# Segment sums of the first eleven tiles moved beside the FFN, their left factors moved into the steps, and the first ten steps reordered

## The chip, the cores and the metric

The kernel runs on one core of a Trainium2 chip. The metric is device time in microseconds: the median of several executions. A separate execution is profiled, and every row quoted here is from that one. The engines are called TensorE (PE, its weight loads PEld), VectorE (DVE), ScalarE (ACT), GpSimd (POOL) and SyncE (SP, which only issues transfers).

## The reference

One layer of a recurrent model for x of 4 batches, 256 positions and 512 features. xn is the layer norm of x. The mixer projects xn with in_proj_w to a gate (8192 wide), to xBC (8192 + 2 x 1024) and to dt (128 heads). xBC goes through a causal convolution of four taps and a silu. Then, with heads of 64 and eight groups that share B and C:

```python
dt = softplus(dt + dt_bias); Adt = -exp(A_log) * dt
L = exp(segment_sum(Adt))            # decay from position j to position i
Y_diag = (C B^T * L) @ (x * dt)      # inside a chunk
Y_off = C @ states * exp(cumsum(Adt))  # from the chunk before
y = (Y_diag + Y_off + D * x) * silu(gate)
y = group_rms_norm(y) * norm_w
out = x + (y @ out_proj_w.T) * silu(FFN(xn))
```

The FFN has ternary weights of width 1792 with a scale for each row. The kernel uses chunks of 128 positions, two for each batch, in place of the reference's 32, which gives the same sums. `segment_sum` of a head is a running sum of Adt from each key position to each later query position.

## The kernel before

The work has two stages in program order: a front, and then 66 steps.

**The front** (`front`) makes the layer norm, the FFN, dt with its sums, and B and C with their scores for the eight groups. The FFN is the backbone: 28 FFN steps (two halves of the tokens by fourteen blocks of 128 features), each with 8 gate matmuls, 8 up matmuls and 8 down matmuls; the down matmuls are those of the FFN step before. Everything else is cut into pieces of generators, and the loop takes one piece, `next(pieces)`, at three places of each FFN step. One such call is a turn: 84 turns lie in the FFN, and what is left over runs after it. `all_pieces` says which generator starts at which turn. `dt_pieces` starts at turn 6; it writes the rows of Adt (`rows`, in DRAM) at turn 17. `bc_pieces(g)`, the projection chain of a group, starts at turn 11 + 8g and has 14 pieces, so two chains overlap. In its first four pieces four matmul products add into one PSUM bank `px`, and after each ScalarE copies the bank into `cpad` or `xpad` (L424) before the next product may add. Later pieces add `pz` and `pq` (L434, L437, L440), and then VectorE runs three convolution taps on `cT` and three on `bT` (L181), which read `cpad` and `xpad`; the copies of the next chain wait for these reads. Pieces 11 to 13 make the scores (L460) that go to DRAM. `early_pieces` starts at turn 20. For each of eleven tiles it loads two blocks of in_proj_w, makes four sums of 128 x 256 from them in two turns (L142 to L146, the left factors of a Strassen-like product) and stores them in DRAM in `early`; one tile takes five turns.

FFN results leave through `hl` (L565, a VectorE difference that the next down matmuls need), `sg` (L548), and `ffn_out` (L301, L302).

**The steps.** Step i (0 to 65) projects tile i (of 64, two heads each), while tile i - 1 goes through the state-space part and tile i - 2 through gating; from step 10 on (`og >= 0`) the output projection of an earlier group runs in it too, three or four products a step (L721). The projection is seven products of four matmuls of 128 x 512 (L173) in PSUM banks `px`, `pq` and `pz`, which several products share: `px` is copied by ScalarE (`pz` L822, `gT` L832, `xpad` L846 and L877) between products, and `pq` is added to `xpad` by VectorE (L869) before its second product may add to it.

For tile i - 1, two rows of Adt are loaded with a broadcast to 128 partitions (`load_rows`, tiles `m` of 128 x 1024). Each is turned into the segment sums by one VectorE scan (`decay_scan`, L612), exponentiated on ScalarE (`decay_exp`, L615) and multiplied by the scores (`meet`, L618 and L619). `y_begin` (L651) puts D * x in the bank `py`; `values_0` and `values_1` transpose x (L624) and scale it (v0 and v0t at L632, v1 at L641); `y_products` (L665) is 48 small matmuls in 12 pairs. `last_tap` (L177, ScalarE) and three taps (L181) make the convolution of tile i, `conv_silu` its silu. `yg` (L672) gates tile i - 2, and `Square` (L857, L860) feeds the norm.

The scans of step i are one in the middle of the step and one at its end. In steps 0 to 10 the left factors of the next tile are read from `early` (transfers L803 and L914); from step 11 on `combine_w` makes them at the end of the step with four sums.

Nothing is scheduled by a planner: inside `tc.manual_schedule()` each engine runs its instructions in the order of the program. SP issues the transfers in program order too, and waits in place when a transfer needs a result or a free buffer; POOL issues the accumulating transfers and casts the FFN weights.

Of the kernel before, what the change touches and what calls it, by code (L numbers as in the profile page):

```python
# [81 lines left out]
def mixer_ffn(ctx: ExitStack, tc: tile.TileContext, x, in_w, conv_w, conv_b, dt_bias, a_log, d_col,  # L82
# [101 lines left out]
    def conv_silu(i, xT):  # L184
        xf = xT.rearrange("p b l -> p (b l)")
        nc.scalar.activation(xf, xf, AF.Silu, bias=cb[:, i:i + 1])


    def front(pre, one_of, fp, f2, hp, wq):
        ones = one_of.tile([P, P], F32, name="ones")  # L190
# [384 lines left out]
    with (tc.manual_schedule(), tc.tile_pool(name="pre", bufs=NT) as pre,  # L575
          tc.tile_pool(name="one_of", bufs=1) as one_of, tc.tile_pool(name="fp", bufs=3) as fp,
          tc.tile_pool(name="f2", bufs=2) as f2, tc.tile_pool(name="hp", bufs=1) as hp,
          tc.tile_pool(name="wq", bufs=1) as wq):
        a = front(pre, one_of, fp, f2, hp, wq)

# [14 lines left out]
    def load_rows(ct):  # L595
        ms = []
        for h in range(2):
            m = mp.tile([P, T], F32, name="m")
            nc.sync.dma_start(m, rows[2 * ct + h, 0:T].partition_broadcast(P))
            ms.append(m)  # L600
        return ms

    def load_off(ct):
# [5 lines left out]
        return offs  # L609

    def decay_scan(m):
        nc.vector.tensor_tensor_scan(m, m, after, 0.0, ALU.add, ALU.mult)  # L612

# [40 lines left out]

    def y_products(ps, vs, ms, offs):
# [4 lines left out]
        for b in range(NB):  # L660
            py = ps[b // 2][:, b % 2, :]
            for q, v, stop in ((0, v0, True), (1, v1, False), (1, v0t, True)):
                for h, d in enumerate(halves):
                    m = off[h][:, b, :] if v is v0t else diag[h][:, b, q, :]
                    nc.tensor.matmul(py[d, q * P:(q + 1) * P], v[:, b, h, :], m,  # L665
                                     start=False, stop=stop, skip_group_check=True)

# [93 lines left out]
    with tc.manual_schedule():  # L761
        nc.sync.dma_start(gm, scores[0])
        ms, offs = {0: load_rows(0)}, {0: load_off(0)}
        xTs, gTs, yps, wos, rights, toms = {}, {}, {}, {}, {}, {}
        sqacc = rs = ya = outs = left = nxt = ob = sa = sb = sc = None
        for i in range(CT + 2):
# [62 lines left out]
            if here:  # L829
# [3 lines left out]
                if lead:  # L833
                    decay_exp(ms[i - 1][1])
                if i:
                    decay_scan(ms[i][0])
                product(pz, a12, x21, False)
            if old:
                meet(ms[i - 1][0], offs[i - 1][0])
                meet(ms[i - 1][1], offs[i - 1][1])  # L840
                if r == 0 and here:
                    nc.sync.dma_start(gm, scores[g])
                yps[i - 1] = y_begin(i - 1, xTs[i - 1])
            if here:
                product(px, s3, t3, False)
                nc.scalar.copy(xpad_h[1], by_batch(px))  # L846
# [6 lines left out]
            if older:  # L853
                yf = yg.rearrange("p b l -> p (b l)")
                if (i - 2) % PER_G == 0:
                    sqacc = sqp.tile([P, T], F32, name="sqacc")
                    nc.scalar.activation(sqacc, yf, AF.Square)  # L857
                else:
                    sq = sqp.tile([P, T], F32, name="sq")
                    nc.scalar.activation(sq, yf, AF.Square)  # L860

# [13 lines left out]
            if here:  # L875
                product(px, a22, t4, False)
                nc.scalar.copy(xpad_h[0], by_batch(px))  # L877
                if i == 0:
                    decay_scan(ms[i][0])
                    decay_scan(ms[i][1])  # L880
                product(pq, s4, x22, False)
            if old and og < 0:
                vs.append(values_1(i - 1, xTs[i - 1]))
            if here:
                nc.vector.tensor_add(gT[:, HALF:], gT[:, HALF:], pq)  # L885
                if og >= 0 and on == 0:
                    rs = small.tile([P, NT], F32, name="rs2", bufs=2)
                    nc.vector.reciprocal(rs, sd)
            if old and og >= 0:
                vs.append(values_1(i - 1, xTs[i - 1]))  # L890
            if here:
                xTs[i] = xtp.tile([P, NB, L], F32, name="xT")
# [7 lines left out]
            if old:  # L900
                y_products(yps[i - 1], vs, ms.pop(i - 1), offs.pop(i - 1))
            if older and (i - 2) % PER_G:
# [132 lines left out]
```

## Time and profile before

| what | us |
|---|---|
| runs: median (lowest to highest of 3) | 1793.18 (1792.14 to 1793.36) |
| the profiled execution's own time | 1795.49 |
| its span, first to last instruction | 1793.0 |
| TensorE busy in the span | 1742.7 (97%) |
| VectorE busy in the span | 1448.6 (81%) |
| ScalarE busy in the span | 1066.0 (59%) |
| the 128 scans `m<-m,after`, VectorE | 292.0, 2282 ns each |

A group row reads: line, engine, operation, out<-in, shape, count, then busy us and the mean ns of one, then the engine's idle time before it and who ended it. A row of waits reads: who waited, for whom, us in total, times, longest. A row of stretches reads: from:to, length, then for PE, PEld, DVE, ACT and POOL the busy us and number of instructions, then the granted TensorE clock (1.00 is full), the busy share of the DMA engines and GB/s. A timeline row reads: start us, length us, engine, line, operation, tiles, shape, count, and in brackets the idle time before it and what ended it. The stretches of the steps are cut in the middle of each step's first product.

### The profile page before, as it was taken

Reading aid. Unit: us, or ns where it says so; the run is one execution under the profiler, and the core shown is the slowest. Engines: PE = TensorE matmul, PEld = TensorE weight load, DVE = VectorE, ACT = ScalarE, POOL = GpSimd, SP = SyncE. Lnnn points to the kernel's source line nnn. Section 1 sums busy time; section 2 is a strip of 40 time slices with the busy share of each in tenths; the row PEclk is TensorE's granted clock in tenths of the full one; section 3 lists DMA queues with packets and bytes.
Section 4 is the critical chain, followed back from the end, with each engine's and each line's share of the span. In section 5 each row is a group of like instructions: output and inputs, shape, how many; then the busy total and the mean of one; then the engine's idle time right before and its main releaser. Section 6 shows DMA issues by size and latency. Waiting matters only on the chain.

```text
span 1793.0 us, 22592 instructions
## 1 busy us (share of the span) xinstructions
PE 1742.7 (97%) x8494; PEld 1117.4 (62%) x8494; DVE 1448.6 (81%) x1740; ACT 1066.0 (59%) x1417; POOL 197.3 (11%) x239
## 2 busy tenths in 40 slices
PE   9999999999899999999999999999999999999989
PEld 6566666455466666666666666666666666666667
DVE  5758675799988888888888888888888888888846
ACT  4544343577666666666666666666666666666630
POOL 3221221000000000111011101110111011101110
PEclk9999999999999999999999999999999999999989
DMA  6254643566846665767676767676777676766674
GB/s 223 80 185 155 212 162 123 196 223 215 253 138 203 195 210 178 201 197 210 180 202 197 210 182 203 197 208 185 203 197 209 185 203 197 208 185 203 179 211 141
DMA packets 164235, 342.69 MB, mean 191 GB/s; under 512 B 15392, under 2 KB 55968, under 8 KB 164128
## 3 DMA queue, kind: packets, MB, share of 16 engines
q1 hardware_dynamic: 141296, 287.78, 46.3%
q0 software_dynamic: 22832, 53.49, 16.8%
q8 instruction: 67, 1.10, 0.2%
q14 instruction: 40, 0.33, 0.1%
HBM read 236.08 MB, written 76.28 MB: 174 GB/s over the span
## 4 chain that ended last, share of the span: by engine, by line
PE 89%; DVE 6%; ACT 4%; issue 1%; DMA 1%; ACTq 0%; DVEq 0%; SPq 0%
PE px L173 27%; PE po L721 21%; PE pq L173 13%; PE py L665 9%; PE pz L173 7%; PE pp L285 4%; PE pf L293 2%; ACT xpad L846 2%; PE tp L624 2%; PE pg L460 1%; DVE cT L181 1%; PE pv L683 1%; DVE xT L181 1%; DVE bT L181 1%; DVE m L612 0%
## 5 line engine op out<-in xcount | busy, mean ns | idle before, releaser
L173 PE MATMUL px<-xc,w 128*128 128x512 f32 x576 | 278.7, 606 | 19.4 <-ACT xpad L846 14.1
L612 DVE TENSOR_TENSOR_SCAN m<-m,after 128x1024 f32<-128x1024 f32 x128 | 292.0, 2282 | 0.0
L181 DVE SCALAR_TENSOR_TENSOR xT<-xpad,cw,xT 128x1024 f32<-128x1024 f32 x192 | 246.2, 1282 | 4.6
L173 PEld LDWEIGHTS px<-xc,w 128*128 128x128 f32 x576 | 104.2, 190 | 136.3 <-issue 97.4
L721 PE MATMUL po<-wo,ya 128*128 128x256 f32 x768 | 178.4, 382 | 0.0
L665 PE MATMUL py<-m,v 128*64 128x128 f32 x2048 | 162.2, 278 | 3.9 <-DVE v L641 3.9
L618 DVE TENSOR_TENSOR m<-m,gm 128x1024 f32<-128x1024 f32 x128 | 154.8, 1209 | 8.9 <-ACT m L615 8.9
L721 PEld LDWEIGHTS po<-wo,ya 128*128 128x128 f32 x768 | 142.6, 192 | 17.6 <-issue 0.3
L904 POOL DMA_DIRECT2D sqacc<-sq x55 | 46.9, 853 | 931.1 <-ACT sq L860 927.3
L173 PE MATMUL px<-xc,s 128*128 128x512 f32 x288 | 137.5, 600 | 5.0 <-ACT pz L822 2.2
L173 PE MATMUL px<-xnT,w 128*128 128x512 f32 x288 | 141.9, 615 | 0.0
L173 PE MATMUL pq<-xnT,s 128*128 128x512 f32 x288 | 136.2, 595 | 1.1 <-DVE xpad L869 1.1
L615 ACT ACTIVATE m<-m 128x1024 f32<-128x1024 f32 x128 | 135.4, 1058 | 0.7
L173 PE MATMUL pq<-xc,s 128*128 128x512 f32 x288 | 135.4, 592 | 0.3 <-DVE gT L885 0.3
L173 PE MATMUL pz<-xnT,w 128*128 128x512 f32 x288 | 135.3, 592 | 0.0
L665 PEld LDWEIGHTS py<-m,v 128*64 128x64 f32 x2048 | 118.0, 138 | 26.2 <-issue 19.7
L721 PE MATMUL po<-tw,sy 128*128 128x256 f32 x512 | 117.1, 382 | 1.2 <-ACT sa L775 1.2
L869 DVE TENSOR_TENSOR xpad<-xpad,pq 128x512 f32<-128x512 f32 x64 | 43.7, 683 | 80.3 <-ACT xpad L846 80.3
L721 PEld LDWEIGHTS po<-tw,sy 128*128 128x128 f32 x512 | 98.1, 192 | 15.2 <-ACT sa L775 1.6
L624 PEld LDWEIGHTS tp<-ident,xT 128*128 128x128 f32 x512 | 64.3, 143 | 67.8 <-issue 67.2
L672 DVE TENSOR_TENSOR yg<-py,gT 128x512 f32<-128x512 f32 x128 | 83.8, 678 | 22.7 <-PE py L665 22.7
L173 PEld LDWEIGHTS px<-xc,s 128*128 128x128 f32 x288 | 54.7, 192 | 73.0 <-issue 65.8
(172 smaller groups left out, 3059.8 us busy)
## 6 DMA issues: line engine op xcount, KB each, us to landing
m<-rows SPq DMA_DIRECT2D x128, 512.0 KB, 6.4
w<-in_in_w SPq DMA_DIRECT2D x133, 256.0 KB, 6.8
mo<-rows SPq DMA_DIRECT2D x128, 256.0 KB, 7.2
gated<-yg SPq DMA_DIRECT2D x64, 512.0 KB, 8.2
ya<-gated SPq DMA_DIRECT2D x30, 1024.0 KB, 7.1
sqacc<-sq POOLq DMA_DIRECT2D x55, 512.0 KB, 5.4
wo<-in_out_w SPq DMA_DIRECT2D x64, 256.0 KB, 7.1
acc<-sa POOLq DMA_DIRECT2D x24, 512.0 KB, 5.9
```

Of the source, the lines that this page charges most:

```text
L173: nc.tensor.matmul(pp, a[:, k, :], b[:, k, :], start=start and k == 0, stop=k == KT // 2 - 1, skip_group_check=not start)
L181: nc.vector.scalar_tensor_tensor(xT, xpad[:, :, k:k + L], cw[:, i, k:k + 1], xT, ALU.mult, ALU.add)
L285: nc.tensor.matmul(pp, w[:, k * P:(k + 1) * P], part[:, k, :], start=(k == 0 and part is xh), stop=(k == KT - 1 and part is xl))
L612: nc.vector.tensor_tensor_scan(m, m, after, 0.0, ALU.add, ALU.mult)
L615: nc.scalar.activation(m, m, AF.Exp)
L618: nc.vector.tensor_mul(m, m, gm[:, 0:T])
L624: nc.tensor.transpose(tp[:, b, :], xT[:, b, c * P:(c + 1) * P], ident)
L665: nc.tensor.matmul(py[d, q * P:(q + 1) * P], v[:, b, h, :], m, start=False, stop=stop, skip_group_check=True)
L672: nc.vector.tensor_mul(yg[:, 2 * i:2 * i + 2, :], ps[i], by_batch(gT[:, i * HALF:(i + 1) * HALF]))
L721: nc.tensor.matmul(po, a[:, k, :], b[:, k, :], start=start and k == 0, stop=k == HG - 1, skip_group_check=not start)
L869: nc.vector.tensor_add(xpad_h[1], xpad_h[1], by_batch(pq))
L904: nc.gpsimd.dma_start(sqacc, sq, accum_op=ALU.add)
```

## The change

`early` now holds 22 tiles of 128 x 1024: the segment sums of the 22 rows (two heads of eleven tiles). `early_pieces` starts at turn 18. At every third turn it loads one row of Adt with a broadcast into a buffer of the pool `ep` (two of them, as large in all as the pool `wq` that goes), runs the scan on the row loaded three turns before, and stores it. The 23rd round falls on turn 84, after the FFN. In the steps `load_rows` reads these tiles for the first eleven tiles of the mixer, the scans up to step 10 go, and every step loads both blocks of its weights whole.

In the first ten steps (`fill`) the order changes: the square comes ahead of the copy of `xpad`, `y_begin` behind it; the four sums for the next tile are made in the step, two before the first tap and two after the last; `last_tap` and the first tap come ahead of `values_1`; and `y_products` does the products with v0 and v0t of all batches before those with v1. Step 10 makes its sums with `combine_w` as later steps do. Every matmul of `y_products` has stop=True.

```diff
-    early = dram.tile([EARLY, P, 4, KT // 2, P], F32, name="early")
+    early = dram.tile([2 * EARLY, P, T], F32, name="early")
...
         def early_pieces():
-            for n in range(EARLY):
-                w = wq.tile([P, 2, KT, P], F32, name="wq")
-                for m, i in enumerate((n + 1, CT + n + 1)):
-                    nc.sync.dma_start(w[:, m], in_w[i])
-                for _ in range(2):
+            ms = {}
+            for n in range(2 * EARLY + 1):
+                if n < 2 * EARLY:
+                    ms[n] = ep.tile([P, T], F32, name="em")
+                    nc.sync.dma_start(ms[n], rows[n, 0:T].partition_broadcast(P))
+                if n:
+                    m = ms.pop(n - 1)
+                    decay_scan(m)
+                    nc.sync.dma_start(early[n - 1], m)
+                for _ in range(3):
                     yield
-                s = wq.tile([P, 4, KT // 2, P], F32, name="sq")
-                yield from combine_to(s[:, 0], s[:, 1], s[:, 2], s[:, 3], w)
-                nc.sync.dma_start(early[n], s)
-                yield
...
-                if turn == 20:
+                if turn == 18:
                     later.append(early_pieces())
...
-            nc.sync.dma_start(m, rows[2 * ct + h, 0:T].partition_broadcast(P))
+            n = 2 * ct + h
+            nc.sync.dma_start(m, early[n] if ct < EARLY else rows[n, 0:T].partition_broadcast(P))
...
+        parts = [(0, v0), (1, v1), (1, v0t)]
+        order = [(b, *p) for b in range(NB) for p in parts]
+        if last_v1:
+            order = [(b, *parts[n]) for ns in ((0, 2), (1,)) for b in range(NB) for n in ns]
...
-            if i + 1 <= EARLY:
-                w = wp.tile([P, 2, KT, P], F32, name="w")
-                nc.sync.dma_start(w[:, 0], in_w[i + 1])
-                nc.sync.dma_start(w[:, 1, 0:2], early[i, :, 3])
-                nc.sync.dma_start(w[:, 1, 2:4], in_w[CT + i + 1, :, 2:4])
-            elif i + 1 < CT:
+            fill = og < 0
+            if i + 1 < CT:
                 w = load_w(i + 1, CT + i + 1)
...
-                if i:
+                if i >= EARLY:
                     decay_scan(ms[i][0])
...
-                yps[i - 1] = y_begin(i - 1, xTs[i - 1])
+                if not fill:
+                    yps[i - 1] = y_begin(i - 1, xTs[i - 1])
...
+            if older and fill:
+                square()
             if here:
                 product(px, s3, t3, False)
                 nc.scalar.copy(xpad_h[1], by_batch(px))
+            if old and fill:
+                yps[i - 1] = y_begin(i - 1, xTs[i - 1])
...
-                if i == 0:
-                    decay_scan(ms[i][0])
-                    decay_scan(ms[i][1])
                 product(pq, s4, x22, False)
-            if old and og < 0:
-                vs.append(values_1(i - 1, xTs[i - 1]))
+            if fill:
+                s = scp.tile([P, 3, KT // 2, P], F32, name="s")
+                sums = combine_to(s[:, 0], s[:, 1], s[:, 2], blocks(w)[2], w)
+                a = factors(w, s)
+                next(sums)
+                xTs[i] = xtp.tile([P, NB, L], F32, name="xT")
+                last_tap(i, xTs[i], xpad)
+                conv_taps(i, xTs[i], xpad, (0,))
+                if old:
+                    vs.append(values_1(i - 1, xTs[i - 1]))
...
-                conv_taps(i, xTs[i], xpad)
+                conv_taps(i, xTs[i], xpad, (1, 2) if fill else (0, 1, 2))
...
-                if i + 1 <= EARLY:
-                    s = scp.tile([P, 3, KT // 2, P], F32, name="s")
-                    nc.sync.dma_start(s, early[i, :, 0:3])
-                    a = factors(w, s)
+                if fill:
+                    next(sums)
                 elif i + 1 < CT:
                     a = combine_w(w)
...
-                if i:
+                if i >= EARLY:
                     decay_scan(ms[i][1])
```

More of the change, by code (lines that the diff above doesn't have):

```diff
@@ L186, in conv_silu, with decay_scan, front @@
         nc.scalar.activation(xf, xf, AF.Silu, bias=cb[:, i:i + 1])
-    def front(pre, one_of, fp, f2, hp, wq):
+    def decay_scan(m):
+        nc.vector.tensor_tensor_scan(m, m, after, 0.0, ALU.add, ALU.mult)
+    def front(pre, one_of, fp, f2, hp, ep):
         ones = one_of.tile([P, P], F32, name="ones")
@@ L577, in mixer_ffn @@
           tc.tile_pool(name="f2", bufs=2) as f2, tc.tile_pool(name="hp", bufs=1) as hp,
-          tc.tile_pool(name="wq", bufs=1) as wq):
-        a = front(pre, one_of, fp, f2, hp, wq)
+          tc.tile_pool(name="ep", bufs=2) as ep):
+        a = front(pre, one_of, fp, f2, hp, ep)
     xtp = main.enter_context(tc.tile_pool(name="xtp", bufs=2, reuse_waits="tile"))
@@ L659, in y_products @@
         halves = [slice(h * HD, (h + 1) * HD) for h in range(2)]
-        for b in range(NB):
-            py = ps[b // 2][:, b % 2, :]
[L662 to L666, printed above, removed]
+        parts = [(0, v0), (1, v1), (1, v0t)]
+        order = [(b, *p) for b in range(NB) for p in parts]
+        if last_v1:
+            order = [(b, *parts[n]) for ns in ((0, 2), (1,)) for b in range(NB) for n in ns]
+        for b, q, v in order:
+            py = ps[b // 2][:, b % 2, :]
+            for h, d in enumerate(halves):
+                m = off[h][:, b, :] if v is v0t else diag[h][:, b, q, :]
+                nc.tensor.matmul(py[d, q * P:(q + 1) * P], v[:, b, h, :], m, start=False,
+                                 stop=True, skip_group_check=True)
     def y_gate(ps, gT):
@@ L842, in mixer_ffn, with square @@
                     nc.sync.dma_start(gm, scores[g])
-                yps[i - 1] = y_begin(i - 1, xTs[i - 1])
+                if not fill:
+                    yps[i - 1] = y_begin(i - 1, xTs[i - 1])
+            def square():
+                nonlocal sq, sqacc
+                yf = yg.rearrange("p b l -> p (b l)")
+                first = (i - 2) % PER_G == 0
+                sq = sqp.tile([P, T], F32, name="sqacc" if first else "sq")
+                nc.scalar.activation(sq, yf, AF.Square)
+                if first:
+                    sqacc = sq
+            if older and fill:
+                square()
             if here:
@@ L852, in mixer_ffn @@
                     nc.scalar.mul(wo, wo, nw[:, wg * PER_G + k:wg * PER_G + k + 1])
[L853 to L860, printed above, removed]
+            if older and not fill:
+                square()
             if og >= 0 and (here and on % 2 == 0 or i == CT - 1):
@@ L888, in mixer_ffn @@
                     nc.vector.reciprocal(rs, sd)
-            if old and og >= 0:
+            if old and not fill:
                 vs.append(values_1(i - 1, xTs[i - 1]))
-            if here:
+            if here and not fill:
                 xTs[i] = xtp.tile([P, NB, L], F32, name="xT")
```

8 lines of the change are left out of this document (3 added, 5 removed).

## The prediction

> **What bounds the kernel now.** I read the head of the page first, then the waits of TensorE, then a table of stretches cut at the steps, then the queues of VectorE and ScalarE around single stalls.
>
> ```profile
> span 1793.0 us, 22592 instructions
> PE 1742.7 (97%) x8494; PEld 1117.4 (62%) x8494; DVE 1448.6 (81%) x1740; ACT 1066.0 (59%) x1417; POOL 197.3 (11%) x239
> ```
>
> TensorE is busy 97% and the change leaves its products as they are, so time can only come from its 50 us of idling and from halved clock. The stretches (length, then busy time by engine, clock, DMA) show where that is: one row for the front from its sixth FFN step on, then steps 0, 1, 2, 9, 10 and 11.
>
> ```profile
> 67.42:311.23 243.81, 234.80 (x942) 160.27 (x941) 163.10 (x218) 95.77 (x131) 51.36 (x63) 1.00 0.48 166
> ```
>
> ```profile
> 311.23:324.19 12.96, 12.28 (x30) 5.24 (x29) 5.71 (x6) 5.79 (x10) 2.37 (x4) 1.00 0.78 291
> 324.19:346.13 21.94, 18.57 (x86) 9.14 (x84) 16.84 (x18) 11.95 (x15) 0.00 (x0) 0.92 0.28 105
> 346.13:363.39 17.26, 16.61 (x85) 8.64 (x84) 15.88 (x17) 12.39 (x15) 0.00 (x0) 1.00 0.50 175
> 467.00:485.40 18.40, 16.61 (x85) 8.64 (x84) 18.14 (x19) 12.39 (x15) 0.85 (x1) 1.00 0.85 257
> 485.40:514.08 28.68, 26.46 (x133) 17.05 (x132) 24.42 (x27) 18.98 (x24) 0.00 (x0) 0.94 0.35 122
> 514.08:535.63 21.55, 21.31 (x109) 13.21 (x108) 17.65 (x20) 14.93 (x21) 0.84 (x1) 1.00 0.68 221
> ```
>
> Steps 2 to 8 all take 17.27. A later step has three or four output products more; they differ by 23.27 - 21.55 = 1.72, so step 11 without its three would take 16.4: that is the floor of a step, and steps 2 to 8 lose 0.86 each. Step 9 loses 2.0, step 1 5.5, step 10 4.2 (step 18, of the same work, takes 24.5): 17.7 us to be won at most. The waits in steps 2 to 8, and then those of the front:
>
> ```profile
> PE py L665 <- DVE v L641: 2.9, 7, 0.4
> PE px L173 <- ACT xpad L846: 1.7, 7, 0.2
> ```
>
> ```profile
> PE px L173 <- ACT xpad L424: 2.9, 2, 1.6
> PE px L173 <- ACT cpad L424: 2.0, 2, 1.1
> PE pf L293 <- DVE hl L565: 1.7, 1, 1.7
> PE pg L460 <- ACT bT L186: 1.3, 2, 0.8
> ```
>
> The front's stalls are few, but all are of one kind: a ScalarE copy or VectorE result comes late because VectorE is in a burst of convolution taps, although VectorE is idle for 80.7 of the 243.8 us. One such burst (the queue of VectorE, then one row of ScalarE):
>
> ```profile
> 226.25 2.61 DVE L181 SCALAR_TENSOR_TENSOR cT<-cpad,cw,cT 128x1024 f32<-128x1024 f32 x2 [2.38 <-ACT cT L177]
> 228.77 0.83 DVE L142 TENSOR_TENSOR sq<-wq 128x256 f32<-128x256 f32 x1
> 229.64 0.43 DVE L143 TENSOR_TENSOR sq<-sq,wq 128x256 f32<-128x256 f32 x1
> 229.98 0.75 DVE L548 SCALAR_TENSOR_TENSOR sg<-pp,us,sg 128x512 f32<-128x512 f32 x1
> 230.64 1.28 DVE L181 SCALAR_TENSOR_TENSOR cT<-cpad,cw,cT 128x1024 f32<-128x1024 f32 x1
> ```
>
> ```profile
> 232.03 0.59 ACT L424 COPY cpad<-px 128x512 f32<-128x512 f32 x1 [0.65 <-DVE cT L181]
> ```
>
> The third tap on cT must end before ScalarE may overwrite cpad, and TensorE's next product waits for that copy (1.06 us here). So what is put between the second and third tap is paid in full.
>
> **The change, part by part.**
>
> *VectorE in the front.* Out go 44 small sums (groups L142, L143, L145, L146 on sq: 5.9, 5.8, 5.0, 4.6 = 21.3 us); in come 22 scans at 2.2 (2282 ns each, overlapping their neighbours by 0.08): 48.4. VectorE gets 27 us more where it has 80.7 idle. Bounds: 0 if all fits, 27 if every added microsecond is paid. I go through the eight projection chains, with the scan every third turn:
> - Chain at 82: the first row load waits on SP for the landing of adt (3.0 us after 73.67), so the chain's w, issued from 75.86, comes 1.3 later. VectorE waits for it already (0.94 us at 81.62); the stall of 1.29 at 84.88 becomes 2.6: +1.3.
> - Chain at 116: a scan before the last tap on bT in place of two sums; that tap ends 117.1, not 115.9, and xpad's copy had no slack: +1.2.
> - Chains at 141 and 233: the scan stands between second and third tap, where 1.1 to 1.2 us of sums stood: +1.1 and +1.0; the stalls become 2.1.
> - Chain at 170 to 180: a scan after the first tap on bT, and one before the four xl differences: +1.3; the stall of 1.6 becomes 2.5 with 0.4 ahead of it.
> - Chain at 209: +0.8 (a slack of 1.2 against about 2). Chain at 269: 0, the last tap is later by 0.6 and had 1.0.
> - Last chain: the scan goes before the last tap at 293.67; bT's silu and the score product at 296.5 come 2.4 later: +2.4, a stall of 3.2.
>
> Sum 9.1. Then the clock: the product at 333.34, after 2.45 us of idling, and that at 490.35, after 2.25, take 3.68 in place of 1.98, at a clock of 0.54; after 1.7 us (286.25:293.67, clock 1.00) nothing drops. Three of my stalls exceed 2.2 and two lie just under. The drops came at 2.2 or more, but I have two cases only, so I count two drops of 1.7: +3.4, between 0 and 8.5. The front costs 12.5.
>
> [...]
>
> [...] Taps take 1372 and 1347 ns there and 1282 in the steps, but the one scan there (L350) takes 2285 beside 2282. [...]
>
> *DMA in the front.* 22 loads and 22 stores of 512 KB replace 22 loads of 256 and 11 stores of 512: 11 MB more on 40.6. DMA share 0.48, stores land in 2.9, row loads in 4.9; a buffer of ep turns in 2.2 + 2.9 + 4.9 = 10 us against two FFN steps (16 or more). Hidden behind the FFN steps; what stands behind a waiting store on SP are the FFN's loads two steps ahead. If landing doubled, VectorE would wait some 3 us in the shortest steps.
>
> *Step 0 and 1.* SP stands at the store of the last scan, which follows the four L301 (to 312.52): 314.8 in place of 312.55 for the second m load. The w loads, issued at 313.89 and landing in about 7 to 8 under a full DMA, go out at 316.5 and land near 324 to 324.8; step 1's first product wants them at 323.33. Behind w stand the two sums, tap 0 and gT's addition: pq comes free at 327.2 (325.4 before). The two scans of step 0 are gone, so the taps end at 329.8 against 329.2. The chain that ended in gT's copy (silu 1.15, table load 1.28, exp 1.06, copy 0.57) ends at 333.9, 0.6 later than before. But the idling comes in three pieces of 0.6 to 1.8, so I expect no halved clock (-1.7), and the v1 wait goes (-0.6, and 0.2 at pq): -1.9. I take -1.5; bounds -5.5 (the floor) and +1.5 (clock drops all the same, or w is 1 us later).
>
> *Steps 2 to 8.* VectorE loses two scans (-4.4) and gains four sums (+1.6); xpad's addition no longer delays pq's second product (0.2), and products with v1 go last. v1 now stands behind tap 0, so behind ScalarE's last_tap. In step 4: xpad copied at 389.2, then y_begin 1.25, two wo multiplications 1.3, copy 0.55, last_tap 1.1, tap 0 1.3, v1 0.65: 395.3. TensorE starts y at 393.3 and has 8 pairs of 0.217 before v1: 395.0, a wait of 0.3. With one wo multiplication (5 to 8) or none (2) v1 is ready 0.1 to 0.3 before. So 5 x 0.86 + 2 x 0.55 = -5.4; bounds -6.0 and 0, if last_tap takes the place of the wait. The two sums wait for the w issued some 1.5 us into the step, which lands by 9, while they come up at 11.5: hidden behind the meets; were it late, tap 0, v1, gT and so y and pq would wait. The rows read back from early are 512 KB as before, and the load of s (384 KB a step) goes. The square replacing y_begin ahead of xpad's copy (1.04 for 1.29) cost nothing, as ScalarE then waits for the product; the stop flags cost nothing. POOL's queue keeps its order.
>
> *Steps 9 and 10.* right_factors' two sums (1.2 each) stand before tap 0 and v1: v1 waits 1.0, xpad's addition 0.2; step 9 gains 0.8. The taps end 2.1 after step 10's start (1.8 before), so pz's copy in step 10 is later by 0.3: +0.4, with half a chance that the clock holds: -0.9. Bounds: -6.2 and +1.
>
> **Sum.** Front +12.5; steps -1.5 - 5.4 - 0.8 - 0.5 = -8.2: +4.3. The profiled execution took 1795.49 (span 1793.0 and 2.5 around it) and would take 1799.8; it stands 2.3 over the median of 1793.18, so the median comes to 1797.5.
>
> **The rivals.** (a) Faster: VectorE's idle time in the front swallows the scans. For it: 80.7 us of idling, and copies into cpad that were late in two chains of eight only. It decides where the front costs under 8.2. With 3 in the front and 9 won it gives 1787. (b) The steps don't move: last_tap replaces v1's wait, the w of step 1 is late, and the front costs its 12.5: 1806. For it: margins of 0.1 to 0.3 in my schedule. (c) Both balance: 1793. Differences under 0.2% (3.6 us) can't be told from none.
>
> **How the numbers follow.** Forecast (1794 to 1803) 0.45, rival (a) 0.22, (b) 0.20, (c) 0.13. Of (a) 0.2 lies beyond -3.6; of the forecast about 0.08 and all of (c) within; so faster 0.20, same 0.22, slower 0.58. The range goes from a front that costs 4 with 11 won (1786) to a front of 18 with 3 won (1808).
>
> **What would show it.** Right: front longer by 9 to 13 with stalls on L424's copies over 2 us; steps 2, 5 to 8 at 16.4, 3 and 4 at 16.7; step 10 still over 27. Wrong: a front within 4 us of its old length; step 10 at 24.5; steps 2 to 8 at 17.

## The result and the profile after

| | before | after |
|---|---|---|
| median (lowest to highest of 4 runs), us | 1793.24 (1792.14 to 1793.36) | 1809.28 (1806.78 to 1811.48) |
| profiled execution: own time, span | 1795.49, 1793.0 | 1811.48, 1809.8 |

The changed kernel is slower: 1.0090 of the time before, with a 95% interval from 1.0073 to 1.0108. The difference of the medians is 16.0 us where the prediction had 4.3, and the time lies 1.3 us above its range.

The head of the page of after:

```profile
span 1809.8 us, 22583 instructions
PE 1747.3 (97%) x8494; PEld 1122.9 (62%) x8494; DVE 1446.3 (80%) x1740; ACT 1067.4 (59%) x1417; POOL 208.8 (12%) x239
```

TensorE has the same 8494 products and needs 4.6 us more for them; VectorE's total hardly moves. Next the stretches of after, cut as for before: the front from its sixth FFN step on, then steps 0, 1, 2, 9 and 10 (from:to, length, busy time of PE, PEld, DVE, ACT and POOL with instructions, clock, DMA share, GB/s):

```profile
67.77:335.29 267.52, 243.85 (x942) 165.10 (x940) 190.81 (x195) 96.44 (x131) 62.80 (x63) 0.97 0.55 191
...
335.29:350.30 15.01, 12.52 (x30) 5.15 (x29) 4.60 (x6) 5.80 (x10) 2.37 (x4) 1.00 0.89 309
350.30:369.62 19.32, 16.66 (x86) 8.59 (x85) 15.44 (x22) 12.08 (x15) 0.00 (x0) 1.00 0.20 79
369.62:385.99 16.37, 16.13 (x86) 8.75 (x85) 12.96 (x19) 12.39 (x15) 0.00 (x0) 1.00 0.45 162
484.61:502.02 17.41, 16.57 (x85) 8.65 (x84) 15.09 (x21) 12.39 (x15) 0.85 (x1) 1.00 0.79 243
502.02:530.91 28.89, 26.47 (x133) 16.99 (x132) 20.34 (x30) 18.97 (x24) 0.00 (x0) 0.94 0.25 92
```

The front takes 267.52 where it took 243.81: +23.7. Of this, 9.05 is TensorE's own busy time (234.80 to 243.85, at a clock of 0.97 in place of 1.00), and 14.7 is idling (9.0 to 23.7). VectorE's work there grew by 27.7. The steps gained: steps 0 and 1 together 34.90 to 34.33, steps 2 to 8 120.87 to 115.0, step 9 18.40 to 17.41; step 10 lost 0.2. From step 0 to the end the kernel is 7.3 shorter. So the steps did nearly what was forecast (-8.2), and the front cost twice its 12.5.

The waits of TensorE in that front of after, and then its wait in steps 2 to 8:

```profile
PE px L173 <- ACT xpad L427: 10.2, 5, 3.7
PE px L173 <- ACT cpad L427: 6.2, 4, 2.5
PE pg L463 <- ACT bT L186: 4.0, 2, 3.5
PE pf L296 <- DVE hl L570: 3.1, 2, 2.0
```

```profile
PE px L173 <- ACT xpad L861: 1.7, 7, 0.2
```

They are the same four waits as before (2.9, 2.0, 1.3 and 2.8 us in the same stretch), grown by 14.5 together. In steps 2 to 8 the wait for v1 is gone, and only the 0.24 for xpad is left in each step.

### The profile page after: what moved, and what is told of

It reads as the page before. It is cut to its first block, busy times and chain, and to the rows that moved or that the text cites. A ratio compares the mean times of both kernels' runs of the same rounds, so it can differ in the third digit from the quotient of the medians.

```text
span 1809.8 us, 22583 instructions
## 1 busy us (share of the span) xinstructions
PE 1747.3 (97%) x8494; PEld 1122.9 (62%) x8494; DVE 1446.3 (80%) x1740; ACT 1067.4 (59%) x1417; POOL 208.8 (12%) x239
## 3 DMA queue, kind: packets, MB, share of 16 engines
q0 software_dynamic: 22832, 53.49, 16.7%
## 5 line engine op out<-in xcount | busy, mean ns | idle before, releaser
L189 DVE TENSOR_TENSOR_SCAN m<-m,after 128x1024 f32<-128x1024 f32 x106 | 241.8, 2282 | 0.0
L727 PEld LDWEIGHTS po<-tw,sy 128*128 128x128 f32 x512 | 97.1, 190 | 15.8 <-ACT sa L781 1.4
```

The source lines that it names most:

```text
L727: nc.tensor.matmul(po, a[:, k, :], b[:, k, :], start=start and k == 0, stop=k == HG - 1, skip_group_check=not start)
```

## Where the front's time went

One stall shows what the forecast had not seen: the chain at 170 to 190, where TensorE waits 3.75 for one copy into xpad. SP's queue first, then VectorE's, then ScalarE's with the copy (start, length, engine, line, operation, tiles, shape, count, idle time before):

```profile
180.44 0.33 SPq L482 DMA_DIRECT2D early<-em  x1
180.86 1.21 SPq L133 DMA_DIRECT2D w<-in_in_w  x2
```

```profile
177.72 2.69 DVE L189 TENSOR_TENSOR_SCAN em<-em,after 128x1024 f32<-128x1024 f32 x1
180.34 0.72 DVE L553 SCALAR_TENSOR_TENSOR sg<-pp,us,sg 128x512 f32<-128x512 f32 x1
180.98 1.27 DVE L181 SCALAR_TENSOR_TENSOR bT<-xpad,cw,bT 128x1024 f32<-128x1024 f32 x1
184.77 0.42 DVE L142 TENSOR_TENSOR s<-w 128x256 f32<-128x256 f32 x1 [2.52 <-DMA w<-in_in_w]
...
185.57 1.28 DVE L181 SCALAR_TENSOR_TENSOR bT<-xpad,cw,bT 128x1024 f32<-128x1024 f32 x1
```

```profile
188.09 0.63 ACT L305 ACTIVATE xt<-xt 128x512 f32<-128x512 f32 x1 [5.89 <-DVE xt L304]
189.19 0.58 ACT L427 COPY xpad<-px 128x512 f32<-128x512 f32 x1
```

The store of a tile of `early` stands in SP's queue directly behind its scan, and the scan ends at 180.41. The load of the chain's next weights (`w`, L133) stands behind that store and so goes out at 180.86, 2.1 us after the start of its FFN step (178.77); in the kernel before, it went out at 163.75, 8.0 ahead of that step's start (171.73):

```profile
163.75 0.96 SPq L133 DMA_DIRECT2D w<-in_in_w  x2
```

VectorE comes to the sums that need `w` at 182.25 and waits 2.52. Behind these sums in its queue stand the last tap on bT, `hl` and the first `xt` of the FFN's output (L304, 187.37). The copy into xpad needs the tap, which ends at 186.85; but ScalarE comes to the silu of that `xt` (L305) first and waits for VectorE's `xt` until 188.09, so the copy starts at 189.19. All of this stands behind the wait for `w`. The wait for `w` occurs three times in this front (2.86 at 83.9, this one, and 2.63 at 284.9); before, there was one of 0.9. The waits of VectorE and of SP in the front of after:

```profile
DVE s L142 <- DMA w<-in_in_w: 8.0, 3, 2.9
```

```profile
SPq L482 <- DVE em L189: 135.6, 18, 10.0
```

SP stood 136 us of this front at stores that waited for a scan. In the kernel before it stood 85 us at stores of the sums too, but there it did not hold the `w` of these two late chains, those at 170 and at 280 (the forecast's chain at 269): they went out at 163.75 and 255.73, 8.0 and 7.8 ahead of their FFN steps, between two stores (152.30 and 174.38, 250.28 and 268.36). The `w` of the chain at 82 is late for another reason: the first row load, ahead of it, waits for `adt` to land, as forecast.

## The experiments

The theory after the result had three parts. *Bursts*: a scan costs what of it stands between VectorE's taps and the copy that waits for them, and nothing elsewhere. *Queue*: SP's order makes `w` late. *Clock*: a long stall also halves the clock for a while (0.50 from 190.51 to 193.92 in after, behind the stall of 3.75). The rivals: that the scans or the transfers cost by their number alone (contention for memory or the DMA engines), wherever they stand; and for the steps, that leaving out the scans brings the gain, and not the new order.

**Stores one round later.** The scans stay in the same turns as in after; each store goes out one round (three turns) later, and for that there are three buffers.

```diff
-            for n in range(2 * EARLY + 1):
+            for n in range(2 * EARLY + 2):
+                if n > 1:
+                    nc.sync.dma_start(early[n - 2], ms.pop(n - 2))
                 if n < 2 * EARLY:
...
-                if n:
-                    m = ms.pop(n - 1)
-                    decay_scan(m)
-                    nc.sync.dma_start(early[n - 1], m)
+                if 0 < n <= 2 * EARLY:
+                    decay_scan(ms[n - 1])
...
-          tc.tile_pool(name="ep", bufs=2) as ep):
+          tc.tile_pool(name="ep", bufs=3) as ep):
```

> The changed kernel, but each row's store is issued one round (three turns) after its scan, and ep has a third buffer, so SP no longer stands in its queue until the scan is done. The changed kernel's trace shows w of a projection chain issued at 180.86 and 280.91, each right behind a store that waited for its scan, and VectorE waiting 2.5 and 2.6 us for those w. Queue theory (the loss beyond my forecast is SP's wait): those two waits go, the stalls of 3.7 and 1.6 us behind them shrink by 1 to 2.5 each, one or two halved clocks go, the front is 5 to 8 us shorter: about 1802. Burst theory alone (the scans between the taps are all of it): no change beyond 1.5 us: 1808 to 1810.

Measured: 1802.27 (1799.64 to 1803.92), 1.0048 of before (1.0034 to 1.0061). SP's queue and the waits of VectorE for `w` in this kernel:

```profile
172.27 0.46 SPq L477 DMA_DIRECT2D early<-em  x1
172.82 0.46 SPq L480 DMA_DIRECT2D em<-rows  x1
173.33 1.38 SPq L133 DMA_DIRECT2D w<-in_in_w  x2
```

```profile
DVE s L142 <- DMA w<-in_in_w: 2.7, 1, 2.7
```

The `w` of the chain at 170 goes out 7.4 us ahead of the start of its FFN step (180.78 here), where it went out 2.1 behind it, and of the three waits one is left, that of the chain at 82. The FFN step with the stall of 3.75 goes from 21.48 to 17.18, that at 280 from 16.54 to 14.55. SP's order is worth 7.0 us of the time, and 8.0 of the front in the profiles. Of these 8.0, these two FFN steps give 6.3. The last chain gives 2.8 more, while FFN steps 12 and 20 change by +2.0 and -1.6; no `w` was late there, and what changed is whether the clock was halved behind a stall (behind that of step 20 it ran at 1.00 from 247.52 to 250.94, where after has 0.50) and which scans have casts of GpSimd beside them (their mean is 2338 ns, and 2432 in after; see the last section). The clock and the casts were not tried apart, nor was the third buffer apart from the later stores.

**The same without the scans; and nothing early at all.** Two kernels: the one above without `decay_scan` in `early_pieces`, and one without `early_pieces` whose steps read `rows`; neither makes the segment sums of the first eleven tiles anywhere.

```diff
-                if 0 < n <= 2 * EARLY:
-                    decay_scan(ms[n - 1])
```

> As the one before (stores a round later, three buffers), but the 22 scans in the front are left out: the rows go to DRAM as they were loaded, so the outputs of the first eleven tiles differ. Transfers are as before. Burst theory: VectorE's 50 us in the front were the cost, so the front returns to within 3 us of its length before the change (243.8 from the sixth FFN step to step 0) and the whole takes 1785 to 1789. Contention theory (the 22 MB of extra loads and stores slow the chains' loads): the front stays 6 us or more longer than before, 1792 or more.

> The front does no early work at all, neither sums nor scans nor their transfers; the first eleven tiles use the rows unsummed (scans left out, so their outputs differ). Steps as in the changed kernel. This is what the steps alone are worth: -7.5 us by the changed kernel's steps against those of before. All theories: 1783 to 1787; below 1785 the four sums of the old early work had a price in the front too (two stalls of 0.9 and 1.1 us stood behind them).

Measured: 1783.64 (1782.35 to 1783.95) and 1780.97 (1779.21 to 1781.41). With the lengths of the front from the start of FFN step 7 (77.96 in after) to step 0, this takes the price of the front apart:

| kernel | front, us | median, us |
|---|---|---|
| nothing early | 229.15 | 1780.97 |
| 22 loads and stores, no scans | 231.94 (+2.8) | 1783.64 (+2.7) |
| with the scans | 249.37 (+17.4) | 1802.27 (+18.6) |
| stores right behind the scans (after) | 257.33 (+8.0) | 1809.28 (+7.0) |
| before, with its 44 small sums | 233.62 | 1793.24 |

The transfers by their number cost nearly nothing. Their 2.8 lie in one place, the chain at 82 (its FFN step grows by 3.2), where the first row load waits on SP for `adt` to land and `w` stands behind it (stall 2.97 against 1.38, and a halved clock, which took the other 1.6). The early work of the kernel before, sums with their loads and stores, had cost 4.5 in the front (233.62 against 229.15), so that without SP's part the exchange costs 2.8 + 17.4 - 4.5 = 15.7.

**The scans in other turns.** A chain has eight turns from one to the next. Turns 0 to 3 hold its products with the copies into cpad and xpad, 6 and 7 the first taps, and 0 and 1 of the next chain the last two taps on bT; in a turn the scan comes behind the chain's piece. The kernels here load three rows at once, make the three scans in three turns that follow one another, and store the three tiles together; the number that differs is the turn in which `early_pieces` starts. There are three buffers here too. The kernels with turns 1 to 3, 2 to 4 and 4 to 6 also have the edit to step 9 below, which leaves the program of the front as it is; the one with turns 6, 7 and 0 has not.

```diff
+            for n in range(0, 2 * EARLY, 3):
+                ms = {}
+                for k in range(n, min(n + 3, 2 * EARLY)):
+                    ms[k] = ep.tile([P, T], F32, name="em")
+                    nc.sync.dma_start(ms[k], rows[k, 0:T].partition_broadcast(P))
+                for _ in range(2):
+                    yield
+                for k in range(n, n + 3):
+                    if k in ms:
+                        decay_scan(ms[k])
+                    yield
+                yield
+                for k, m in ms.items():
+                    nc.sync.dma_start(early[k], m)
+                for _ in range(2):
+                    yield
...
-                if turn == 18:
+                if turn == 20:
```

> The changed kernel with the same 22 scans, but three in each cycle of a projection chain, in the turns 3, 4 and 5 of each cycle of eight, where VectorE waits for the score, pz and pq products; their loads come behind the chain's w, their stores two turns after the last scan, ep has three buffers. Burst and queue theory: the same work of VectorE costs little there, the front is 1 to 5 us longer than before the change and step 0's w is not late: 1786 to 1791, faster than before. If VectorE's added time itself is what costs, wherever it stands: 1800 or more.

> The same kernel and the same number of loads, scans and stores, in the same groups of three, but three turns later: the scans come in turns 6, 7 and 0 of a chain's eight, where VectorE is in the convolution taps. The burst theory (a scan costs what of it stands between a tap and the copy that waits for that tap; elsewhere nothing) expects each of the seven chains to pay one to two scans of 2.3 to 2.7 us, some with a halved clock: a front 12 to 25 us longer than the placed kernel's 298, and 1797 to 1810. The theory that the placed kernel is faster because its transfers are grouped and its stores late, whatever the turn, expects 1785 to 1788.

> The kernel with the late right-factor sum, its cycle of loads, scans and stores begun one turn earlier: scans in turns 2 to 4 of a chain's eight in place of 3 to 5. In the trace with 3 to 5 the third scan of a group (162.22, 2.68 us) ends 1.3 us after ScalarE's part of the convolution is ready and so pushes the taps; hl and xt come late (TensorE waits 1.1 and 2.3 us, one of them with a halved clock; 2.4 again near 287). The burst theory expects these waits to shrink, since turn 2 comes behind the last tap on bT: 2 to 4 us less in the front, 1780 to 1783. If those waits have another cause, the time stays at 1784 to 1785.

> The same, begun one turn later than with 3 to 5: scans in turns 4 to 6. The third scan of each group then stands directly ahead of the taps and ScalarE's part is ready before it: the burst theory expects each of the seven chains to pay 1 to 2.5 us more for it where it pays 0 to 2 now, 4 to 14 us in all with halved clocks: 1788 to 1798. If only scans between two taps cost anything, the time stays at 1784 to 1786.

> The same, begun two turns earlier: scans in turns 1 to 3. The first scan of each group then stands between the second and third tap on bT, and the copy into xpad waits for the third. The burst theory expects a full scan, 2.3 to 2.7 us, in chains without slack there and about 1.5 in the others, against the gain of start_19 at the other end of the group: 6 to 14 us over start_19. If it is the number of scans in a group and not their turn that matters, the time equals that of start_19.

| scans in turns | front, us | median, us | ratio to before (95%) |
|---|---|---|---|
| 1 to 3 | 245.2 | 1796.41 | 1.0014 (1.0004 to 1.0024) |
| 2 to 4 | 232.7 | 1780.80 | 0.9932 (0.9917 to 0.9947) |
| 3 to 5 | 235.8 | 1784.26 | 0.9948 (0.9935 to 0.9960) |
| 3 to 5, without the edit to step 9 below | 233.7 | 1785.52 | 0.9953 (0.9940 to 0.9965) |
| 4 to 6 | 250.0 | 1803.39 | 1.0060 (1.0041 to 1.0079) |
| 6, 7 and 0, without that edit | 268.6 | 1818.88 | 1.0141 (1.0125 to 1.0156) |

The same 22 scans, loads and stores cost the front between 3.5 and 39 us over none at all, by their turn alone. So neither their number nor contention by number sets the price. The two late groups cost more than expected, as TensorE's waits for hl come on top (12.6 us in six waits with turns 6, 7 and 0, 11.0 in four with turns 4 to 6). From turns 3 to 5 to turns 2 to 4, the waits for hl shrank as expected (1.1 to none near 165, 2.4 to 1.1 near 287), while that for xt stayed (2.3 and 2.6). VectorE in a burst of the kernel with turns 6, 7 and 0, and then in the same chain with turns 2 to 4:

```profile
246.63 2.61 DVE L181 SCALAR_TENSOR_TENSOR cT<-cpad,cw,cT 128x1024 f32<-128x1024 f32 x2 [2.37 <-ACT cT L177]
249.16 2.69 DVE L189 TENSOR_TENSOR_SCAN em<-em,after 128x1024 f32<-128x1024 f32 x1
251.77 0.72 DVE L558 SCALAR_TENSOR_TENSOR sg<-pp,us,sg 128x512 f32<-128x512 f32 x1
252.42 1.48 DVE L181 SCALAR_TENSOR_TENSOR cT<-cpad,cw,cT 128x1024 f32<-128x1024 f32 x1
253.81 1.27 DVE L181 SCALAR_TENSOR_TENSOR bT<-xpad,cw,bT 128x1024 f32<-128x1024 f32 x1
255.01 2.28 DVE L189 TENSOR_TENSOR_SCAN em<-em,after 128x1024 f32<-128x1024 f32 x1
```

```profile
226.38 2.61 DVE L181 SCALAR_TENSOR_TENSOR cT<-cpad,cw,cT 128x1024 f32<-128x1024 f32 x2 [2.38 <-ACT cT L177]
228.91 0.75 DVE L558 SCALAR_TENSOR_TENSOR sg<-pp,us,sg 128x512 f32<-128x512 f32 x1
229.57 1.28 DVE L181 SCALAR_TENSOR_TENSOR cT<-cpad,cw,cT 128x1024 f32<-128x1024 f32 x1
230.76 2.60 DVE L181 SCALAR_TENSOR_TENSOR bT<-xpad,cw,bT 128x1024 f32<-128x1024 f32 x2
```

Between the second and third tap on cT stand 3.3 us in the first kernel and 0.7 in the second, and TensorE waits 2.66 for cpad there against nothing.

Turns 1 to 3 were expected to be bad for another reason than the one found. The first scan does stand behind the last tap on bT, so it delays no copy into xpad. What is late is `w` again: in this kernel the three loads go out in turn 7, one turn ahead of the `w` of the next chain, so it stands behind them; with turns 2 to 4 they go out in the same turn as `w`, and behind it. SP's queue with turns 1 to 3, VectorE's wait there, and SP's queue with turns 2 to 4:

```profile
77.02 1.28 SPq L478 DMA_DIRECT2D em<-rows  x3
78.40 1.64 SPq L133 DMA_DIRECT2D w<-in_in_w  x2
```

```profile
86.61 0.42 DVE L142 TENSOR_TENSOR s<-w 128x256 f32<-128x256 f32 x1 [5.58 <-DMA w<-in_in_w]
```

```profile
75.08 0.89 SPq L133 DMA_DIRECT2D w<-in_in_w  x2
76.08 1.59 SPq L478 DMA_DIRECT2D em<-rows  x3
```

That FFN step takes 24.32 in the one and 16.49 in the other, 7.8 of the 12.5 us between the two fronts. Part of the wait is the later issue (3.3 us); the rest goes with a later landing behind 1.5 MB of rows (7.3 us from issue in the first kernel, 4.5 in the second). Behind the long stall, TensorE's 5.9 for xpad, the clock is halved for 6.83 us.

**The order of the steps, and the scans in them.** Two kernels take the steps' gain apart. The first is the one with the scans in turns 3 to 5, with `fill` false throughout: the order of the later steps, sums made at the end of the step, and still no scans in steps 0 to 10. The second is the one with turns 2 to 4 in the new order, but with nothing early and the two scans back in each step.

```diff
-            fill = og < 0
+            fill = False
```

```diff
-EARLY = 11
+EARLY = 0
```

> The kernel with the scans placed in turns 3 to 5 of a chain's cycle, but steps 0 to 9 in the order of the later steps: the square behind xpad's copy, y_begin ahead of it, all four sums made by combine_w at the end of the step, values_1 behind gT's addition. The scans of these steps stay out. If the new order is what takes 0.9 us from each of steps 2 to 8 (v1 was the last thing that y_products waited for), they go back to 17.0 to 17.3, step 1 to 20 or more, and the time is 4 to 7 us over the placed kernel's 1785.5: 1790 to 1792. If leaving out the two scans is enough by itself (VectorE is freed of 4.6 us a step and gets 3.2 of sums back), steps 2 to 8 stay at 16.4 to 16.6 and the time at 1785 to 1787.

> The kernel of start_19 with nothing made early: no loads, scans or stores beside the FFN, and the two scans of each of steps 0 to 10 back in the steps, in the new order with its four sums there too. The front should be as short as that of no_early (229 us from FFN step 7 on, 3.5 less than start_19's 232.7). VectorE in steps 2 to 8 then has 12.95 + 2 x 2.28 = 17.5 us of work in steps that take 16.4 now. If VectorE becomes the bound, these steps take 17.5 to 18.5, +1.1 to +2.0 each, and steps 0, 1, 9 and 10 lose 1 to 3 each: 1788 to 1797. If the order alone is what brings the gain and the scans fit under the waits, steps 2 to 8 stay under 16.8 and the time is 1777 to 1781, which would make the early scans needless.

Measured: 1792.45 (1790.84 to 1793.65) and 1787.83 (1785.04 to 1788.45). One of the steps 2 to 8 in each (first the old order without scans, then the new order with them), and what TensorE waits for in these seven steps:

```profile
348.08:365.24 17.16, 16.34 (x85) 8.68 (x84) 13.13 (x19) 12.27 (x15) 0.00 (x0) 1.00 0.43 155
```

```profile
PE py L676 <- DVE v L649: 4.0, 7, 0.6
```

```profile
357.11:374.31 17.20, 16.39 (x86) 8.67 (x84) 17.13 (x21) 13.52 (x17) 0.89 (x1) 1.00 0.70 214
```

```profile
PE pq L173 <- DVE xpad L885: 4.1, 7, 0.7
```

Old order with scans 17.27, old order without 17.16, new order with 17.20, both edits 16.37 to 16.6. In these seven steps neither brings much alone (0.11 and 0.07 a step). Without scans VectorE is busy for 13.1 of 17.2, but v1 stands late in its queue all the same; in the new order with scans VectorE is busy for 17.13 of 17.20 and is the bound, and xpad's addition comes late. The gain of 0.84 a step needs the order, and the order needs the scans out. (The sums that come back into a step are 1.7 us of VectorE by these rows: 15.88 less two scans of 2.28 is 11.3, and 13.0 to 13.1 is measured. The 3.2 of the expectation is too much.)

Outside steps 2 to 8 it is otherwise. In the old order, leaving out the scans alone takes step 9 from 18.40 to 17.5 and step 10 from 28.68 to 26.4, about as far as with the new order in step 9 (17.41), and further in step 10 (27.19, where the stall on pz is 2.42; here it is 1.62). It loses in step 1, 22.35 against 21.94 before and 19.32 in after. And the new order with the scans back in the steps is as a whole 5.9 us faster than before (0.9963, 0.9949 to 0.9977): its front makes nothing early (229.5 against 233.6), and step 1 takes 19.8.

**The second sum of the right factors.** In step 9 it is made behind the taps and not ahead of them (first needed in step 10); the scans are in turns 3 to 5.

```diff
-                if i < CT + 1 and n >= 0 and on == turn:
+                if i < CT + 1 and n >= 0 and on == turn and not (fill and n == 0):
...
                     next(sums)
+                    if on == PER_G - 1 and wg >= 0:
+                        toms[wg].pop(0)()
```

> The placed kernel with one edit: in step 9 the second sum of the right factors (1.2 us on VectorE, first needed in step 10) is made behind the taps and the last two sums rather than ahead of tap 0 and v1. If that sum is what v1 (0.6 us of waiting in step 9) and pz's copy at the start of step 10 (a stall of 2.4 us, which halved the clock in some kernels) wait for, step 9 goes from 17.4 to 16.8, and the time to 1782.5 to 1785. If the taps' own length sets the stall in step 10, the sum only changes places with them (all of it must end before the tables of step 10 are copied): step 10 stays at 27.2 or grows by up to 1.2, and the time stays at 1785 to 1786.5.

Measured: 1784.26 (1783.77 to 1785.2) beside 1785.52 (1783.74 to 1785.8) without it. These times overlap, so the traces must say what the edit does. Step 9 goes from 17.41 to 16.58, since the wait for v1 (0.6) is gone. The stall on pz in step 10 falls only from 2.42 to 2.16. The taps end 1.1 us earlier after the start of step 9 (17.4 for 18.5), but TensorE comes to step 10 earlier too, by 0.83; and behind the last tap ScalarE still has a silu (1.15), a table load (1.28) and an exp (1.06) ahead of the copy into pz. The sum is no longer ahead of it.

The version with turns 2 to 4 and this edit, 1780.80, is faster than both the kernel before and the changed one, and the fastest here that makes all its sums.

## Why the prediction was right and wrong

**The steps: right.** Steps 2 to 8 gave 5.9 (forecast 5.4), at 16.37, and 16.58 and 16.59 in steps 3 and 4 (16.7 expected). Step 9 gave 1.0 (0.8). Steps 0 and 1 gave 0.6 (1.5): the halved clock of step 1 did go (1.00 in its row, where before has 0.92), with its idling in pieces of 1.30 and 1.13, but `w` came 1.81 late in step 0, where I had about 1. Step 10 lost 0.2 (forecast -0.5), its stall grown from 2.22 to 2.42 with the clock halved as before (0.94 in both rows). The 2048 matmuls of `y_products` that read `m` take 278 ns on average before and after, so the stop flags cost nothing. In all -7.3 for -8.2. The reason given, v1's wait, stands by the kernel in the old order, which has that wait and not the gain in steps 2 to 8. For steps 9 and 10 the order was not needed: there that kernel is as fast.

**The front: the kind of wait right, one path missed, and the sum half of what it should be.** VectorE got 27.7 us (forecast 27), and the growth is on the four waits named and in halved clock: 14.5 us of stalls where the forecast had 9.1, and 9.05 of TensorE's busy time where it had 3.4. The terms, in FFN steps (stall before to after, then what the step grew by with the clock):

| term | forecast | stall | grown by |
|---|---|---|---|
| chain at 82 | +1.3 | 1.29 to 3.15 | 3.5 |
| chain at 116 | +1.2 | 0.48 to 1.41 | 1.1 |
| chain at 141 | +1.1 | 0.93 to 2.46 | 1.5 |
| chain at 170 to 180 | +1.3 | 1.60 to 5.07 | 5.7 |
| chain at 209 | +0.8 | 0 to 0.77 | 1.1 |
| chain at 233 | +1.0 | 1.06 to 2.46 | 3.0 |
| chain at 269 | 0 | 0 to 1.62 | 2.3 |
| last chain | +2.4 | 2.53 to 5.44 | 5.5 |
| two halved clocks | +3.4 | | in the steps |

Without SP's part the stalls and clock come to 249.37 - 233.62 = 15.8, against 12.5. So the step that failed first is this sentence: "what stands behind a waiting store on SP are the FFN's loads two steps ahead". The chains' `w` stands behind it too, and for it VectorE waits ahead of its last tap. The chain at 82 was the only one for which I followed `w` through SP's queue. I costed the loads of `early_pieces` and their landing, but moved no other transfer of the front past its stores. Moving the stores gave back 8.0 us of the front, 6.3 of them in "Chain at 170 to 180" (+1.3 for 5.7) and "Chain at 269: 0" (2.3).

Second, the forecast costed a scan at 2282 ns, with the one scan of the front before (L350, 2285) as its support. The scans here:

```profile
L189 DVE TENSOR_TENSOR_SCAN em<-em,after 128x1024 f32<-128x1024 f32 x22 | 53.5, 2432 | 0.0
```

Their mean is 2432 ns, 53.5 us in all, 3.3 more than at the 2282 of the steps (50.2). The 12 scans with no work of GpSimd beside them take 2282 on average; eight that begin while a cast of GpSimd runs take 2691 to 2697, 0.41 us more each. L350 of before, too, begins while a cast runs (77.90 to 81.09), but there the scan took its 2285 and the cast 3.19, where one with nothing beside it takes 0.61.

Third, "I count two drops of 1.7": there were four halved stretches, three of 3.41 us and one of 6.83, 17.1 us at a clock of 0.50, which is about 8.5 us of loss and nearly all of the 9.05 that TensorE's busy time grew by. I had set 8.5 as the upper bound for it.

Of the rivals, (a) failed: VectorE's 80.7 us of idling don't swallow the scans where the change puts them. With the scans in turns 2 to 4 they do, at 3.5 us over none. (b) comes near the measured time (1806), but by luck: the steps did move, which it denied, and the front cost twice what it added. (c) failed too, since the front cost three times what the steps won.

## What to carry to other kernels

Work that is put beside other work costs nothing only where no one waits at that place: the same 22 instructions cost from 3.5 to 39 us by their turn, though VectorE is idle for 22 to 31% of the front in both cases (190.28 busy of 242.88, 193.04 of 278.75), so move them to the turns behind the last use of a shared buffer before judging the idea. A transfer that waits for a result holds up everything issued after it in SP's queue (here a `w` went out 2.1 us behind the start of its FFN step, and VectorE waited 2.52 for it): for each store that is added, list the loads behind it, and ask who waits for them. Where a reorder and a removal come in one change, try each alone: in steps 2 to 8 neither paid without the other, while in steps 9 and 10 the removal paid alone.

## What the runs showed of the hardware that I had not expected

**Stalls and the halved clock.** The length of a stall alone did not decide here whether the clock was halved. After, up to 560 us, the stretches at a clock of 0.50 start at 88.11, 190.51, 248.53, 316.81 and 507.95; that at 316.81 lasts 6.83 us, the others 3.41, and the starts lie 30, 17, 20 and 56 times 3.413 us apart. Before, there are two, at 333.37 and 490.38, which lie 46 times 3.413 apart. After, around FFN steps 12 and 20, which both have a stall of 2.46 on cpad, cut into pieces of 3.413 us counted from those starts (from:to, length, PE busy, ..., clock in the third column from the right):

```profile
142.73:146.14 3.41, 2.19 (x9) 1.31 (x7) 3.41 (x3) 0.62 (x1) 0.00 (x0) 1.00 0.16 65
146.14:149.55 3.41, 2.17 (x6) 1.18 (x7) 3.37 (x4) 2.36 (x4) 0.00 (x0) 1.00 0.90 302
149.55:152.97 3.42, 3.42 (x13) 2.15 (x12) 3.39 (x5) 0.44 (x1) 1.56 (x2) 1.00 0.80 309
...
245.12:248.53 3.41, 1.26 (x3) 0.68 (x4) 3.38 (x4) 2.52 (x4) 0.00 (x0) 1.00 0.88 300
248.53:251.94 3.41, 3.41 (x8) 2.18 (x7) 3.38 (x6) 0.90 (x2) 1.62 (x2) 0.50 1.04 380
```

The first stall falls across two of these pieces with 1.2 of idling each, and the clock holds. The second falls into one, 2.15 idle, and the next runs at 0.50. Over the 13 profiles of this case, from 60 to 560 us and cut like this, all 29 pieces at full clock with 2.09 us or more of idling were followed by one at 0.50 (seven of them before and after, with 2.15 to 2.72), and of the 76 with 1.0 to 1.92 one was (1.87; before and after none of 13, with 1.02 to 1.81). So what a stall of 2.1 to 2.5 cost went by where it fell, and the difference is 1.7 us: the same stall of 2.42 in step 10 made that step 28.89 in after and 27.19 in the kernel with turns 3 to 5. This also makes single profiles of the same work differ: the front with turns 3 to 5, the same with and without the edit to step 9, took 235.8 in one profile and 233.7 in the other, which differ by one halved stretch in the FFN step at 172 (0.50 from 185.26 to 188.67, with the edit).

**A scan and a cast side by side.** After, VectorE's scan at 151.66, and the casts on GpSimd around it (start, length):

```profile
151.66 2.69 DVE L189 TENSOR_TENSOR_SCAN em<-em,after 128x1024 f32<-128x1024 f32 x1
```

```profile
151.41 0.81 POOL L228 CAST wg<-wg_i 128x512 fp32r<-128x512 int32 x1 [8.76 <-DMA wg_i<-in_gate_t]
152.16 2.60 POOL L228 CAST wu<-wu_i 128x512 fp32r<-128x512 int32 x1
```

The scan begins inside the first cast and takes 2.69, 0.41 longer than with no cast beside it; the second cast, 0.61 when nothing is beside it, begins inside the scan, takes 2.60 and ends 0.41 after it. The same returns in the other kernels with early scans: over all nine, 53 casts begin inside one of these scans and outlast it, and 52 of them end 0.41 after it. (The other begins near the scan's end and takes the usual 0.61.) In after there are five, begun 0.84 to 2.19 before the scan's end. TensorE shows no wait for a cast in this front, so only the scan's part of it can have cost time.
